# Attention plus quantised feed-forward on one core: another place for the streamed tiles, an earlier end of the search for the largest product, and another order of roundings

## Chip, core and metric

One core of a Trainium2 chip runs the whole kernel in one launch. The metric is the device time of a run in microseconds; each kernel is timed by the median of its runs.

## The reference

x is (2, 2048, 512), that is 4096 rows of 512. A cross-attention with 128 context rows per batch is added to it, then a feed-forward block whose activations and weights are rounded to integers and scaled back:

```python
x = x + xattn(layernorm(x), ctx_1024, Wq, Wkv)
x = x + ffn(layernorm(x), w_gate, w_up, w_down)

def ffn(x, w_gate, w_up, w_down):
    x = act_qdq(x)                            # 16 bit, one scale over the whole tensor
    up = act_qdq(x @ lpbq_dequant(w_up).T)    # weights: 4 bit, a scale per block of 32
    gate = act_qdq(x @ lpbq_dequant(w_gate).T)
    sig = fixed_qdq_u16(sigmoid(gate))
    gate = act_qdq(gate * sig)
    o = act_qdq(gate * up)
    return o @ lpbq_dequant(w_down).T
```

`act_qdq` takes the largest magnitude of its whole operand, divides by 32767 and rounds. The hidden width is 1536. Each of these scales has to be known before the rounding that uses it, and that cuts the work into stages.

## The kernel before

**Stages.** (1) Norm and attention, in 8 groups of 512 rows (`NG = 8`, `TG = 512`); it leaves the normalised rows, transposed, in `hT`. (2) Gate: per group, 12 chunks of 128 hidden columns. (3) Up: the groups in reverse order, again 12 chunks each; a tile j (0 to 23) is a third of a group, 4 chunks, and has two half tiles c = 2j and 2j+1. (4) Down: 32 units m of 128 rows, two to a tile t of 256 rows.

**Numbers in parts.** TensorE works on exact integers: an activation integer is split into a high and a low part and a third combination (`split_integers`), and so is a weight. A chunk in gate or up is `project`: 8 matmuls of 128x512 into q and 4 into e, with the weights stationary and the activation parts (`parts_g`, `parts_u`) streamed. In down the roles change: the product's parts (`o_parts`) are stationary and the down weights `wd[f]`, f = 0 to 11, are streamed, 24 matmuls into q (L865) and 12 into e (L873).

**Homes.** Group t has its parts in `homes[t % 2]`: `homes[0]` is a pool `parts0` on the left side of SBUF, `homes[1]` is `parts1`, 24 KB per partition and the outermost pool on the right side. In down `homes[1]` holds the weights 0 to 3 (`first_wd`). Ahead of `parts1`, `hT` (64 KB) has stood at that place, and ahead of it `prep0`. The x tiles (`xp`, 4 of 8 KB), the integers `hi` (32 KB) and up's tiles (`keep`: three u of 8 KB and three p of 4 KB) are on the left.

**Up.** Per tile j ACT makes the sigmoid of a later gate tile in three passes (L609 to L611), DVE makes the integers p (L647). Per half tile ACT takes q out of PSUM (L715), DVE subtracts e (L716), the half is stored to `up_d`, and `bound` (ACT L655, DVE L656) takes the largest magnitude of u times p into a column of `pumax`. Only the tile holding the largest of these can hold the largest rounded product. So `fetch_best` finds, per partition, the row of the best half tile, and fetches u and p of it from DRAM with two indirect DMAs (L673). This covers half tiles 0 to 46; half tile 47 is rounded itself. When the scale of u is known (`r_u`, L762), both are rounded (L772), multiplied and reduced (L774), an all-reduce over the partitions follows (L779), and then the scale of the product is known. A flag (L915) says whether the bound was sure; otherwise a general path (not entered here) follows.

**Down.** ACT rounds u to integers (`round_up`, L828); DVE makes the product's integer and its parts (`round_o`, L850, L851, L853, and ACT's cast L854, then `third_part`, L857); TensorE multiplies; `finish_first` (L878, L880) and `finish` (L884) scale, add x and store. The first group's u and p are still on the chip. Later groups load p (L812) and u (`load_up`, L801) from DRAM; u goes into the same three tiles, so a load waits for the last `round_up` that reads them.

**Order.** Each engine runs its queue in order, as laid down by the program's planner at build time. `in_order` adds pairs of instructions of one engine that keep their order without a semaphore; `high_priority` puts a piece ahead in the plan. SP issues nearly all DMAs, in order; POOL issues the two indirect ones. In the first group of down each unit's rounding is made one unit ahead:

```python
if m + 1 < NS * NU:
    ...
    in_order(casts[-1], *round_up(uis[t], tiles_u, t, j * P, P))
    if m + 2 == NS * NU:
        tiles_u = load_up(groups[1])
```

Of the kernel before, what the change touches and what calls it, by code (L numbers as in the profile page):

```python
# [76 lines left out]
def tile_xattn_ffn(  # L77
# [56 lines left out]
    pumax = const.tile([P, NH - 1], F32, name="pumax")  # L134
# [109 lines left out]

    with ExitStack() as c0:

        with ExitStack() as c1:
            prep = c1.enter_context(tc.tile_pool(name="prep", bufs=1))
            xp = c1.enter_context(tc.tile_pool(name="xp", bufs=4))
# [251 lines left out]
        hi_pool = c0.enter_context(tc.tile_pool(name="hi", bufs=1))  # L501
        hi = hi_pool.tile([P, ND, NT], I16, name="hi")
# [20 lines left out]
        with ExitStack() as c2:  # L523
            wg = [load_parts(wg_d, f, "wg") for f in range(NF)]
            s_h, r_h = act_scale(*over_partitions(hmax, name="h"), "h")

            unit = const.tile([P, 1], F32, name="unit")
            nc.vector.tensor_scalar(unit, s_h, BASE, None, ALU.mult)
            wk1 = c2.enter_context(tc.tile_pool(name="wkb1", bufs=1))
            for c in range(ND):  # L530
                nc.vector.tensor_scalar(hi[:, c, :TG], hT[:, c, :TG], r_h, QMAX, ALU.mult, ALU.min)
            first = split_integers(wk1, homes[0], hi[:, :, :TG], [ND, TG], "g0", ND)

            table = const.tile([P, 1], F32, name="table")
            nc.scalar.activation(table, unit, AF.Sigmoid)
            for t in range(1, NG):
                if t % 2:
                    nc.vector.tensor_scalar(hi[:, :, ts(t, TG)], hT[:, :, ts(t, TG)], r_h, QMAX, ALU.mult, ALU.min)
                else:
                    nc.scalar.activation(hi[:, :, ts(t, TG)], hT[:, :, ts(t, TG)], AF.Copy, scale=r_h)  # L540
            hpool.__exit__(None, None, None)
            home1 = tc.tile_pool(name="parts1", bufs=1, side="right")
            homes.append(ctx.enter_context(home1))
            wk2 = c2.enter_context(tc.tile_pool(name="wkb2", bufs=2))
            wpp = c2.enter_context(tc.tile_pool(name="wprep", bufs=1))
            ps_m = c2.enter_context(tc.tile_pool(name="ps_m", bufs=3, space=PSUM))
            ps_t = c2.enter_context(tc.tile_pool(name="ps_t2", bufs=2, space=PSUM))

            steps = chain(split_rows(wpp, ps_t, w_up, wu_d, "u"), split_down(wpp, ps_t))
            groups, wu = {}, []  # L550
            for t in range(NG):
                if t == 0:
                    parts = first
                else:
                    parts = split_integers(wk1, homes[t % 2], hi[:, :, ts(t, TG)], [ND, TG], f"g{t}")
# [24 lines left out]
    keep = ctx.enter_context(tc.tile_pool(name="keep", bufs=NK))  # L580

    with ExitStack() as c3:
# [70 lines left out]
        def bound(c, u, pi):  # L653
            ua = wk2.tile([P, 2, TG], F32, tag="ua", name=f"ua_{c}")
            magnitudes = nc.scalar.activation(ua, u, AF.Abs)  # L655
            nc.vector.tensor_tensor_reduce(ua, ua, pi, 1.0, 0.0, ALU.mult, ALU.max, pumax[:, c : c + 1])  # L656
            return magnitudes

        kept_u, kept_p = [], []
        best = const.tile([P, 8], F32, name="best")  # L660

        def fetch_best():
# [5 lines left out]
            to_row = nc.vector.scalar_tensor_tensor(row, where[:, 0:1], float(P), lane, ALU.mult, ALU.add)  # L668
            fetched = []
            for src, dt in ((up_d, F32), (p_d, I16)):  # L670
# [5 lines left out]
                    in_=src[: NH - 1].rearrange("n p i t -> (n p) (i t)"),  # L676
# [3 lines left out]
            return to_row, *fetched  # L680
# [10 lines left out]
        for j, (t, k) in enumerate(order):  # L691
# [13 lines left out]
            kept_u.append(u4)  # L705
            for h in range(2):
# [3 lines left out]
                if c + 1 < NH:  # L710
# [5 lines left out]
                    nc.vector.tensor_tensor(u4[:, both, :], u4[:, both, :], e, ALU.subtract)  # L716
                else:
                    for i in range(2):
# [4 lines left out]
                        in_order(magnitudes, nc.scalar.activation(v, q, AF.Copy, scale=1.0 + 1.0 / BASE))  # L723
                        in_order(to_row, nc.vector.tensor_tensor(v, v, e, ALU.subtract))
# [42 lines left out]
        two = const.tile([P, 3], F32, name="two")  # L767
        last = [v[:, 2:, :].rearrange("p i t -> p (i t)") for v in (u4, pi)]
        rounded = []
        for i, (uv, pv) in enumerate([last, (ub, pb)]):  # L770
# [3 lines left out]
            nc.vector.tensor_tensor_reduce(product, ui, pv, 1.0, 0.0, ALU.mult, ALU.max, two[:, i : i + 1])  # L774
            if i == 0:
                nc.vector.tensor_scalar(two[:, 2:3], best[:, 1:2], r_u, 1.0 + 2.0**-18, ALU.mult, ALU.mult)
                nc.vector.tensor_scalar(two[:, 2:3], two[:, 2:3], 0.5 * (QMAX + 2.0), None, ALU.add)
        top = const.tile([P, 3], F32, name="top")
        nc.gpsimd.partition_all_reduce(top, two, P, bass_isa.ReduceOp.max)  # L779


    with ExitStack() as c5:
# [14 lines left out]
        def load_up(g):  # L797
            tiles = []
            for k in range(NK):
                u4 = keep.tile([P, NQ, TG], F32, tag="u4", name=f"u5_{g}_{k}")  # L800
                nc.sync.dma_start(  # L801
                    out=u4.rearrange("p (h c) t -> p h c t", h=2), in_=up_d[rows_of(g, k)].rearrange("h p c t -> p h c t")
                )
                tiles.append(u4)
            return tiles
# [19 lines left out]
        def round_up(ui, tiles, t, at=0, width=TD):  # L825
# [4 lines left out]
                    tiles[k][:, :, ds(t % NS * TD + at, width)],  # L830
# [76 lines left out]
        tiles_u, kept_p = kept_u[-NK:], kept_p[-NK:]  # L907
        uis = {0: up_integers(0)}
        in_order(rounded[0], *round_up(uis[0], tiles_u, 0, 0, P))
        scale_of_pu()  # L910
        a_o = const.tile([P, 1], F32, name="a_o")
        nc.vector.tensor_tensor(a_o, top[:, 0:1], top[:, 1:2], ALU.max)
        flag = const.tile([P, 1], I32, name="flag")
        with tc.high_priority():
            nc.vector.scalar_tensor_tensor(flag, top[:, 2:3], floor, a_o, ALU.max, ALU.is_le)  # L915
# [57 lines left out]
        for m in range((last + 1) * NU + 2):  # L973
# [4 lines left out]
            if m <= last * NU + NU - 1:  # L978
# [66 lines left out]
```

## Time and profile before

| what | value |
|---|---|
| median of 3 runs | 1023.36 us (1021.37 to 1025.08) |
| profiled execution | 1021.18 us, its span 1019.4 us |
| PE busy | 953.6 us (94%) |
| DVE, ACT, POOL busy | 806.2, 549.4, 90.4 us |
| granted TensorE clock, mean | 0.975 |
| DMA, mean | 259 GB/s |

Norm and attention take up to about 177 us, gate to about 457, up to 726, down from 743 to the end. In a line of the timeline the columns are the start and the length in us, the engine, the line of the kernel, the operation, the tile written and the tiles read, shapes, a count of merged instructions, and in square brackets the idle time of the engine just before and what ended it. In a line of the waits they are the waiting engine and line, what it waited for, the total in us, how often, and the longest.

### The profile page before, as it was taken

The numbers are of one execution on the slowest core, as the hardware profiler recorded it, in microseconds if no ns is written. First come the engines' busy times: TensorE is split into PE (matmuls) and PEld (weight loads), VectorE is DVE, ScalarE is ACT, GpSimd is POOL, SyncE is SP. The second block draws the span as 40 slices with busy tenths as digits, with TensorE's granted clock in tenths as the row PEclk, the third lists the DMA queues.
The fourth block names the chain that finished last, engine by engine and source line by source line (L and its number), as shares of the span: only waits on it lengthen the run. The fifth ranks groups of instructions, "written<-read, shape, count | busy, mean of one in ns | idle before, by whom it ended". The sixth has DMA issues, their size and how long they took to land. (4 is left out here: it accounts for less than half of the span.)

```text
span 1019.4 us, 11685 instructions
## 1 busy us (share of the span) xinstructions
PE 953.6 (94%) x4321; PEld 764.6 (75%) x4321; DVE 806.2 (79%) x1000; ACT 549.4 (54%) x655; POOL 90.4 (9%) x67
## 2 busy tenths in 40 slices
PE   6998874999999999999999999999488999999998
PEld 5765642888888888878888888888367888888886
DVE  4589865999997989546996997987688997777772
ACT  2268786432333323218997998887255444444331
POOL 0101111000000000000000000000011322222221
PEclk9999997999999999999999999999789999999999
DMA  9187644886895775797997997897946576654711
GB/s 340 32 313 270 253 176 173 332 336 271 311 383 186 300 226 195 254 387 274 352 348 292 344 370 293 334 378 249 393 145 253 185 244 227 237 189 154 243 66 42
DMA packets 103596, 263.72 MB, mean 259 GB/s; under 512 B 6064, under 2 KB 46000, under 8 KB 94832
## 3 DMA queue, kind: packets, MB, share of 16 engines
q1 hardware_dynamic: 102496, 259.02, 68.8%
q0 software_dynamic: 512, 2.88, 0.7%
q10 hardware_dynamic: 528, 1.05, 0.3%
q8 instruction: 34, 0.56, 0.2%
q14 instruction: 26, 0.21, 0.1%
HBM read 136.05 MB, written 126.88 MB: 258 GB/s over the span
## 5 line engine op out<-in xcount | busy, mean ns | idle before, releaser
L517 PE MATMUL q_g<-parts_g,wg 128*128 128x512 f32 x768 | 196.4, 396 | 5.1 <-ACT parts_g L236 5.1
L517 PEld LDWEIGHTS q_g<-parts_g,wg 128*128 128x128 f32 x768 | 144.5, 189 | 38.0 <-ACT parts_g L236 5.5
L568 ACT ACTIVATE g<-q_g 128x512 f32<-128x512 f32 x96 | 57.2, 598 | 182.0 <-PE q_g L517 179.2
L517 PE MATMUL q_u<-parts_u,wu 128*128 128x512 f32 x576 | 144.6, 393 | 0.3 <-ACT u L715 0.3
L517 PEld LDWEIGHTS q_u<-parts_u,wu 128*128 128x128 f32 x576 | 108.2, 188 | 25.2 <-ACT u L715 0.7
L865 PE MATMUL yq<-wd,o_parts 128*128 128x512 f32 x512 | 122.1, 391 | 0.0
L865 PEld LDWEIGHTS yq<-wd,o_parts 128*128 128x128 f32 x512 | 96.6, 189 | 21.1
L521 PE MATMUL e_g<-parts_g,wg 128*128 128x512 f32 x384 | 106.8, 396 | 0.0
L569 DVE CUSTOM_DVE_ANT_0 g<-g,e_g 128x512 f32<-128x512 f32 x96 | 64.8, 681 | 39.2 <-PE e_g L521 38.7
L865 PE MATMUL yq<-first_wd,o_parts 128*128 128x512 f32 x256 | 68.3, 411 | 20.4 <-ACT o_parts L854 20.4
L878 ACT ACTIVATE yqs<-yq,q_o 128x512 f32<-128x512 f32 x32 | 22.0, 687 | 119.1 <-PE yq L865 119.1
L521 PEld LDWEIGHTS e_g<-parts_g,wg 128*128 128x128 f32 x384 | 72.2, 189 | 16.3 <-DVE parts_g L238 0.4
L880 POOL TENSOR_TENSOR qx<-yqs,x 128x512 f32<-128x512 f32 x32 | 64.5, 2016 | 210.6 <-ACT yqs L878 152.0
L521 PE MATMUL e_u<-parts_u,wu 128*128 128x512 f32 x288 | 78.2, 393 | 0.0
L865 PEld LDWEIGHTS yq<-first_wd,o_parts 128*128 128x128 f32 x256 | 50.1, 196 | 32.7 <-ACT o_parts L854 21.0
L857 DVE SCALAR_TENSOR_TENSOR o_parts<-sa,oi 128x1536 fp32r<-128x1536 int16 (+2 forms) x41 | 58.2, 1438 | 19.9 <-PE ye L873 19.9
L656 DVE CUSTOM_DVE_ANT_0 ua<-ua,pi 128x1024 f32<-128x1024 f32 x47 | 57.1, 1220 | 18.8 <-ACT ua L655 18.6
L853 DVE SCALAR_TENSOR_TENSOR o_parts<-sa,oi 128x1536 fp32r<-128x1536 int16 (+2 forms) x41 | 58.6, 1430 | 14.9 <-PE yq L865 13.0
L854 ACT CAST o_parts<-sa 128x1536 fp32r<-128x1536 int16 (+2 forms) x41 | 48.8, 1190 | 34.4 <-DVE sa L851 34.4
L716 DVE TENSOR_TENSOR u<-u,e_u 128x1024 f32<-128x1024 f32 x47 | 57.0, 1217 | 12.4 <-ACT u L715 12.3
L873 PE MATMUL ye<-wd,o_parts 128*128 128x512 f32 x256 | 64.0, 392 | 0.0
L647 DVE SCALAR_TENSOR_TENSOR pi<-gi,k_p,sq 128x2048 int16<-128x2048 int16 x24 | 56.4, 2349 | 9.6 <-ACT sq L611 9.6
(185 smaller groups left out, 1554.5 us busy)
## 6 DMA issues: line engine op xcount, KB each, us to landing
gate_d<-g SPq DMA_DIRECT2D x24, 1024.0 KB, 6.5
up_d<-u SPq DMA_DIRECT2D x48, 512.0 KB, 7.3
gt<-gate_d SPq DMA_DIRECT2D x22, 1024.0 KB, 8.3
u<-up_d SPq DMA_DIRECT2D x21, 1024.0 KB, 6.5
parts_d<-parts_g SPq DMA_DIRECT2D x6, 3072.0 KB, 11.1
parts_u<-parts_d SPq DMA_DIRECT2D x6, 3072.0 KB, 13.4
p_d<-pi SPq DMA_DIRECT2D x24, 512.0 KB, 9.7
p<-p_d SPq DMA_DIRECT2D x84, 128.0 KB, 3.1
```

What stands on the lines that cost most here:

```text
L517: nc.tensor.matmul(q, lhsT=w[:, s, c, :], rhs=parts[:, s, c, :], start=(c + s == 0), stop=(c + s == ND))
L521: nc.tensor.matmul(e, lhsT=w[:, 2, c, :], rhs=parts[:, 2, c, :], start=(c == 0), stop=(c == ND - 1))
L568: nc.scalar.activation(g4[:, i, :], q, AF.Copy, scale=1.0 + 1.0 / BASE)
L569: nc.vector.tensor_tensor_reduce(g4[:, i, :], g4[:, i, :], e, 1.0, LOWEST, ALU.subtract, ALU.max, gtop[:, m : m + 1])
L647: nc.vector.scalar_tensor_tensor(pi, gi, k_p, sq, ALU.mult, ALU.mult)
L656: nc.vector.tensor_tensor_reduce(ua, ua, pi, 1.0, 0.0, ALU.mult, ALU.max, pumax[:, c : c + 1])
L716: nc.vector.tensor_tensor(u4[:, both, :], u4[:, both, :], e, ALU.subtract)
L853: made.append(nc.vector.scalar_tensor_tensor(parts[1][:, c], sa[:, c], -BASE, oi[:, c], ALU.mult, ALU.add))
L857: return nc.vector.scalar_tensor_tensor(parts[2][:, c], sa[:, c], BASE + 1.0, oi[:, c], ALU.mult, ALU.subtract)
L865: nc.tensor.matmul(q, lhsT=parts[s][:, f, :], rhs=wd[f][:, s, :], start=(f + s == 0), stop=(f + s == NF))
L873: nc.tensor.matmul(e, lhsT=parts[2][:, f, :], rhs=wd[f][:, 2, :], start=(f == 0), stop=(f == NF - 1))
L880: nc.gpsimd.tensor_tensor(qx, qs, x1[:, m % NU, :], ALU.add)
```

## The change

x, the integers `hi` and up's tiles get a common pool `far` of four tiles of 8 KB on the right side, opened ahead of all others there, so it is the outermost. `prep0`, `hT` and `parts1` now lie inside it, 32 KB further from the end. Two p tiles share the fourth `far` tile; the third stays in `keep`. The tiles of u are three fixed ones that are written again and again, in up and by `load_up`.

The search for the best product now covers half tiles 0 to 45; the last tile's two halves, 46 and 47, are both rounded from the chip. The search and fetch follow half tile 45, and the subtraction (L716) of half tile 46 comes behind the row on DVE. The older order of half tile 47's instructions behind them goes. The loads of the third parts of the weights 0 to 3 move to the end of up, behind the last store.

In down, unit 0 rounds the second half of tile 0 and then the whole of tile 1, and after that each tile's first unit rounds the next tile. `load_up` of the second group is issued in unit 0 instead of unit 2.

```diff
-    pumax = const.tile([P, NH - 1], F32, name="pumax")
+    pumax = const.tile([P, NH - 2], F32, name="pumax")
...
+    far = ctx.enter_context(tc.tile_pool(name="far", bufs=4, side="right"))
+
+    def far_tile(name):
+        return far.tile([P, NJ * D], F32, tag="far", name=name)
...
-            xp = c1.enter_context(tc.tile_pool(name="xp", bufs=4))
...
-                xt = xp.tile([P, NJ, D], F32, tag="xt", name=f"xt_{g}")
+                xt = far_tile(f"xt_{g}").rearrange("p (j d) -> p j d", j=NJ)
...
-        hi_pool = c0.enter_context(tc.tile_pool(name="hi", bufs=1))
-        hi = hi_pool.tile([P, ND, NT], I16, name="hi")
+        his = [far_tile(f"hi_{i}").bitcast(I16).rearrange("p (t c k) -> p t c k", t=2, c=ND) for i in range(NG // 2)]
+        hi = [his[t // 2][:, t % 2] for t in range(NG)]
...
-    keep = ctx.enter_context(tc.tile_pool(name="keep", bufs=NK))
+    keep = ctx.enter_context(tc.tile_pool(name="keep", bufs=1))
+    tiles_u = [far_tile(f"u4_{i}").rearrange("p (i t) -> p i t", i=NQ) for i in range(NK)]
+    two_p = far_tile("pi_01").bitcast(I16).rearrange("p (n i t) -> p n i t", n=2, i=NQ)
+    kept_p = [two_p[:, 0], two_p[:, 1], keep.tile([P, NQ, TG], I16, name="pi_2")]
...
-            pi = keep.tile([P, NQ, TG], I16, tag="pi", name=f"pi_{j}")
-            kept_p.append(pi)
+            pi = kept_p[j % NK]
...
-                    in_=src[: NH - 1].rearrange("n p i t -> (n p) (i t)"),
+                    in_=src[: NH - 2].rearrange("n p i t -> (n p) (i t)"),
...
-            u4 = keep.tile([P, NQ, TG], F32, tag="u4", name=f"u4_{j}")
+            u4 = tiles_u[j % NK]
...
-                    nc.vector.tensor_tensor(u4[:, both, :], u4[:, both, :], e, ALU.subtract)
+                    less = nc.vector.tensor_tensor(u4[:, both, :], u4[:, both, :], e, ALU.subtract)
+                    if c + 2 == NH:
+                        in_order(row_known, less)
...
-                        in_order(magnitudes, nc.scalar.activation(v, q, AF.Copy, scale=1.0 + 1.0 / BASE))
-                        in_order(to_row, nc.vector.tensor_tensor(v, v, e, ALU.subtract))
+                        nc.scalar.activation(v, q, AF.Copy, scale=1.0 + 1.0 / BASE)
+                        nc.vector.tensor_tensor(v, v, e, ALU.subtract)
...
-                if c + 2 < NH:
+                if c + 3 < NH:
                     bound(c, u4[:, both, :], pi[:, both, :])
-                elif c + 2 == NH:
+                elif c + 3 == NH:
                     with tc.high_priority():
-                        magnitudes = bound(c, u4[:, both, :], pi[:, both, :])
-                        to_row, ub, pb = fetch_best()
+                        bound(c, u4[:, both, :], pi[:, both, :])
+                        row_known, (ub, pb) = fetch_best()
...
-            if t == 0 and k == 1:
-                load_down(range(NE), slice(2, 3))
-
-        rest = load_down(range(NE + NQ, NF), slice(0, 2)) + load_down(range(NE, NF), slice(2, 3))
+
+        rest = load_down(range(NE + NQ, NF), slice(0, 2)) + load_down(range(NF), slice(2, 3))
         in_order(stored, *rest)
...
-        last = [v[:, 2:, :].rearrange("p i t -> p (i t)") for v in (u4, pi)]
+        there = [(u4[:, ts(h, 2), :].rearrange(flat), pi[:, ts(h, 2), :].rearrange(flat)) for h in range(2)]
         rounded = []
-        for i, (uv, pv) in enumerate([last, (ub, pb)]):
+        for i, (uv, pv) in enumerate([*there, (ub, pb)]):
...
-        nc.vector.tensor_tensor(a_o, top[:, 0:1], top[:, 1:2], ALU.max)
+        nc.vector.tensor_reduce(a_o, top[:, 0:3], AX.X, ALU.max)
...
-                if m + 1 < NS * NU:
-                    t, j = divmod(m + 1, NU)
-                    if j == 0:
-                        uis[t] = up_integers(t)
-                    in_order(casts[-1], *round_up(uis[t], tiles_u, t, j * P, P))
-                    if m + 2 == NS * NU:
-                        tiles_u = load_up(groups[1])
-                elif t < last and j == (NU - 1 if t + 1 == NS else 0):
+                if m == 0:
+                    in_order(casts[-1], *round_up(ui, 0, P, P))
+                if j == 0 and t < last:
                     uis[t + 1] = up_integers(t + 1)
-                    in_order(casts[-1], *round_up(uis[t + 1], tiles_u, t + 1))
+                    in_order(casts[-1], *round_up(uis[t + 1], t + 1))
                     if t % NS == NS - 2 and t + NS <= last:
-                        tiles_u = load_up(groups[t // NS + 1])
+                        load_up(groups[t // NS + 1])
```

More of the change, by code (lines that the diff above doesn't have):

```diff
@@ L530, in tile_xattn_ffn @@
             for c in range(ND):
-                nc.vector.tensor_scalar(hi[:, c, :TG], hT[:, c, :TG], r_h, QMAX, ALU.mult, ALU.min)
-            first = split_integers(wk1, homes[0], hi[:, :, :TG], [ND, TG], "g0", ND)
+                nc.vector.tensor_scalar(hi[0][:, c], hT[:, c, :TG], r_h, QMAX, ALU.mult, ALU.min)
+            first = split_integers(wk1, homes[0], hi[0], [ND, TG], "g0", ND)
             table = const.tile([P, 1], F32, name="table")
@@ L537, in tile_xattn_ffn @@
                 if t % 2:
-                    nc.vector.tensor_scalar(hi[:, :, ts(t, TG)], hT[:, :, ts(t, TG)], r_h, QMAX, ALU.mult, ALU.min)
+                    nc.vector.tensor_scalar(hi[t], hT[:, :, ts(t, TG)], r_h, QMAX, ALU.mult, ALU.min)
                 else:
-                    nc.scalar.activation(hi[:, :, ts(t, TG)], hT[:, :, ts(t, TG)], AF.Copy, scale=r_h)
+                    nc.scalar.activation(hi[t], hT[:, :, ts(t, TG)], AF.Copy, scale=r_h)
             hpool.__exit__(None, None, None)
@@ L554, in tile_xattn_ffn @@
                 else:
-                    parts = split_integers(wk1, homes[t % 2], hi[:, :, ts(t, TG)], [ND, TG], f"g{t}")
+                    parts = split_integers(wk1, homes[t % 2], hi[t], [ND, TG], f"g{t}")
                 if t < NG - 2:
@@ L654, in bound @@
             ua = wk2.tile([P, 2, TG], F32, tag="ua", name=f"ua_{c}")
-            magnitudes = nc.scalar.activation(ua, u, AF.Abs)
+            nc.scalar.activation(ua, u, AF.Abs)
             nc.vector.tensor_tensor_reduce(ua, ua, pi, 1.0, 0.0, ALU.mult, ALU.max, pumax[:, c : c + 1])
-            return magnitudes
-        kept_u, kept_p = [], []
         best = const.tile([P, 8], F32, name="best")
@@ L667, in fetch_best @@
             row = const.tile([P, 1], U32, name="row")
-            to_row = nc.vector.scalar_tensor_tensor(row, where[:, 0:1], float(P), lane, ALU.mult, ALU.add)
+            known = nc.vector.scalar_tensor_tensor(row, where[:, 0:1], float(P), lane, ALU.mult, ALU.add)
             fetched = []
@@ L679, in fetch_best @@
                 fetched.append(v)
-            return to_row, *fetched
+            return known, fetched
         def load_down(fs, part=slice(None)):
@@ L701, in tile_xattn_ffn @@
                     load_down(range(NE), slice(0, 2))
-            u4 = keep.tile([P, NQ, TG], F32, tag="u4", name=f"u4_{j}")
+            u4 = tiles_u[j % NK]
             if j:
                 pi = integers_of_p(j)
-            kept_u.append(u4)
             for h in range(2):
@@ L765, in tile_xattn_ffn @@
         nc.vector.tensor_scalar(s_u, s_u, 1.0 / QMAX, TINY, ALU.mult, ALU.max)
-        two = const.tile([P, 3], F32, name="two")
-        last = [v[:, 2:, :].rearrange("p i t -> p (i t)") for v in (u4, pi)]
+        most = const.tile([P, 4], F32, name="most")
+        flat = "p i t -> p (i t)"
+        there = [(u4[:, ts(h, 2), :].rearrange(flat), pi[:, ts(h, 2), :].rearrange(flat)) for h in range(2)]
         rounded = []
-        for i, (uv, pv) in enumerate([last, (ub, pb)]):
+        for i, (uv, pv) in enumerate([*there, (ub, pb)]):
             ui = wk3.tile([P, NQ, TG], I16, tag="gi", name=f"ui_b{i}").rearrange("p i t -> p (i t)")[:, : 2 * TG]
@@ L773, in tile_xattn_ffn @@
             product = wk2.tile([P, 2 * TG], F32, tag="ua", name=f"product_b{i}")
-            nc.vector.tensor_tensor_reduce(product, ui, pv, 1.0, 0.0, ALU.mult, ALU.max, two[:, i : i + 1])
+            nc.vector.tensor_tensor_reduce(product, ui, pv, 1.0, 0.0, ALU.mult, ALU.max, most[:, i : i + 1])
             if i == 0:
[L776 to L779, printed above, removed]
+                nc.vector.tensor_scalar(most[:, 3:4], best[:, 1:2], r_u, 1.0 + 2.0**-18, ALU.mult, ALU.mult)
+                nc.vector.tensor_scalar(most[:, 3:4], most[:, 3:4], 0.5 * (QMAX + 2.0), None, ALU.add)
+        top = const.tile([P, 4], F32, name="top")
+        nc.gpsimd.partition_all_reduce(top, most, P, bass_isa.ReduceOp.max)
     with ExitStack() as c5:
@@ L797, in load_up @@
         def load_up(g):
-            tiles = []
             for k in range(NK):
-                u4 = keep.tile([P, NQ, TG], F32, tag="u4", name=f"u5_{g}_{k}")
                 nc.sync.dma_start(
-                    out=u4.rearrange("p (h c) t -> p h c t", h=2), in_=up_d[rows_of(g, k)].rearrange("h p c t -> p h c t")
-                )
-                tiles.append(u4)
-            return tiles
+                    out=tiles_u[k].rearrange("p (h c) t -> p h c t", h=2),
+                    in_=up_d[rows_of(g, k)].rearrange("h p c t -> p h c t"),
+                )
         def load_p(t):
@@ L823, in up_integers, with round_up @@
             return wki.tile([P, NF, TD], I16, tag="ui5", name=f"ui5_{t}")
-        def round_up(ui, tiles, t, at=0, width=TD):
+        def round_up(ui, t, at=0, width=TD):
             return [
@@ L829, in round_up @@
                     ui[:, ts(k, NQ), ds(at, width)],
-                    tiles[k][:, :, ds(t % NS * TD + at, width)],
+                    tiles_u[k][:, :, ds(t % NS * TD + at, width)],
                     AF.Copy,
@@ L905, in scale_of_o @@
             nc.vector.tensor_scalar(e_o, s_o, -BASE, None, ALU.mult)
-        tiles_u, kept_p = kept_u[-NK:], kept_p[-NK:]
         uis = {0: up_integers(0)}
-        in_order(rounded[0], *round_up(uis[0], tiles_u, 0, 0, P))
+        in_order(rounded[0], *round_up(uis[0], 0, 0, P))
         scale_of_pu()
         a_o = const.tile([P, 1], F32, name="a_o")
-        nc.vector.tensor_tensor(a_o, top[:, 0:1], top[:, 1:2], ALU.max)
+        nc.vector.tensor_reduce(a_o, top[:, 0:3], AX.X, ALU.max)
         flag = const.tile([P, 1], I32, name="flag")
         with tc.high_priority():
-            nc.vector.scalar_tensor_tensor(flag, top[:, 2:3], floor, a_o, ALU.max, ALU.is_le)
+            nc.vector.scalar_tensor_tensor(flag, top[:, 3:4], floor, a_o, ALU.max, ALU.is_le)
         scale_of_o(a_o)
```

## Prediction

> **What bounds the kernel now.** I read the page first, then the PE waits, then PE's timeline group by group, then the timeline of the two places where PE stands still. The page:
>
> ```profile
> span 1019.4 us, 11685 instructions
> PE 953.6 (94%) x4321; PEld 764.6 (75%) x4321; DVE 806.2 (79%) x1000; ACT 549.4 (54%) x655; POOL 90.4 (9%) x67
> PEclk9999997999999999999999999999789999999999
> ```
>
> From 180 us on PE is busy in nearly every slice and its granted clock is full; the exception is near slices 29 to 31 (720 to 785 us). So two things count: the time of one matmul, and what stops PE there. The PE waits name the second; the two stops are 17.1 and 3.2 us:
>
> ```profile
> PE yq L865 <- ACT o_parts L854: 20.4, 2, 17.1
> ```
>
> The first is in PE's timeline. Here is a group whose streamed operand `parts_u` lies in `homes[1]` (t = 1), then one where it lies in `homes[0]` (t = 0). Columns: start us, us.
>
> ```profile
> 665.30 2.04 PE L517 MATMUL q_u<-parts_u,wu 128*128 128x512 f32 x8
> ...
> 668.11 2.03 PE L517 MATMUL q_u<-parts_u,wu 128*128 128x512 f32 x8
> ```
>
> ```profile
> 696.06 1.98 PE L517 MATMUL q_u<-parts_u,wu 128*128 128x512 f32 x8
> ...
> 698.78 1.98 PE L517 MATMUL q_u<-parts_u,wu 128*128 128x512 f32 x8
> ```
>
> The step from one chunk of 12 matmuls to the next (8 of q, 4 of e) is 2.81 us in the odd group and 2.72 us in the even one: 234 against 227 ns a matmul, with the same shapes, full clock and no wait. The weights are the same `wu`; only the home differs. The gate pass shows it too: t = 1 steps from 216.12 to 218.92 (2.80), t = 0 from 192.62 to 195.34 (2.72). In down, where `first_wd` (weights 0 to 3) lies in `homes[1]`:
>
> ```profile
> 808.38 2.03 PE L865 MATMUL yq<-first_wd,o_parts 128*128 128x512 f32 x8
> 810.25 3.81 PE L865 MATMUL yq<-wd,o_parts 128*128 128x512 f32 x16
> ...
> 816.66 2.03 PE L865 MATMUL yq<-first_wd,o_parts 128*128 128x512 f32 x8
> ```
>
> The eight on `first_wd` take 1.87 us (234 ns each), the next 16 take 3.64 (227); a unit of 36 takes 8.28 us, where 36 at 226.7 would take 8.16. So every matmul that streams from `homes[1]` costs some 7 ns (in down, 10 per such matmul) more.
>
> **The change part by part.**
>
> (a) The move. `parts1` (24 KB) is the outermost tile on the right side now; afterwards the four `far` tiles (32 KB) lie outside it, so it ends 32 KB further in. If the slow zone ends there, odd groups run like even ones: gate 4 groups x 12 chunks x 0.08 = 3.8 us; up 48 x 0.09 = 4.3; down 32 units x 0.12 = 3.8. Together 11.9 us, all on the path since PE has no wait in these stages. No row shows f32r data streamed from between the even home and the odd one, so the bounds are 11.9 and 0 (the zone reaches further in). [...] The rows say 234 against 227, so the address or something tied to it matters[...]. [...] I take 11.9.
>
> What replaces it at the end is x, `hi`, u and two tiles of p, which DVE, ACT and DMA touch; PE reads only x there, as the stationary operand of 128 transposes in the first 160 us, where PE waits for others anyway (0). ACT already writes to the right side without loss: L461 into `hT` (64 KB there) takes 991 to 1038 ns for 128x1024, L715 into u on the left 999 to 1029. So 0 for them. The two p tiles in one buffer, u without new tiles and x, `hi`, u sharing buffers all wait for readers one stage or three tiles back: 0, covered by 10.9 us of PE per tile.
>
> The loads of `wg` no longer lie on x's place; they start at 168.78 because the last x was still in use, and can now start some 6 us earlier. PE starts at 176.76 on the chain of maxima and finds its weights: 0.
>
> (b) The end of up. Between the last matmul (723.5) and the first of down:
>
> ```profile
> 729.99 1.07 POOL L673 DMA_INDIRECT best<-up_d,row  x1 [270.09 <-DMA wd<-wd_d]
> 731.37 0.97 POOL L673 DMA_INDIRECT best<-p_d,row  x1 [0.30 <-issue]
> 737.00 1.15 ACT L772 ACTIVATE ui_b<-best,r_u 128x1024 int16<-128x1024 f32 x1 [8.75 <-DMA best<-up_d,row]
> 738.18 1.22 DVE L774 CUSTOM_DVE_ANT_0 product_b<-ui_b,best 128x1024 f32<-128x1024 int16 x1 [8.67 <-ACT ui_b L772]
> ...
> 739.51 0.38 POOL L779 PARTITION_ALL_REDUCE top<-two  x1 [7.17 <-DVE two L774]
> ...
> 742.14 0.48 DVE L850 SCALAR_TENSOR_TENSOR oi<-pi,k_o,ui 128x256 int16<-128x256 int16 x1 [1.17 <-DVEq L918]
> ...
> 743.43 3.78 PE L865 MATMUL yq<-first_wd,o_parts 128*128 128x512 f32 x8 [17.14 <-ACT o_parts L854]
> ```
>
> The gather needs half tile 46 in `up_d`; that store was issued at 720.6 and landed at 729.1, and the gather went out 0.9 later. Now the search stops at half tile 45 (store issued 715.5, landed 723.0) and p of tile 22 (landed 720.6); its row is known by 719, where L656 for 45 ended at 718.9. So the gather goes out at 723.9, 6.1 us earlier. With the same 7.0 us to land it is there at 730.9. Meanwhile r_u is ready at 727.1 and ACT rounds the two halves on the chip: 2 x 1.15, to 729.4. The added half costs 1.15 on ACT and 1.22 on DVE, both under that landing; without that cover, 1.2. Then 1.15 + 1.22 for the fetched one, ending 6.1 us before 739.4. What follows (4.0 us to PE) is unchanged. If the gather lands sooner, ACT's own three roundings end at 730.55 and the gain stops at 7.6; if it meets the `wd` loads as hard as before and loses 2 more, 4. I take 6.1. The bound on 46 that goes (1.05 ACT, 1.22 DVE) lay ahead of the last maxima; L724's order behind the search is gone as well, but the 2.28 us maximum of tile 22 then falls later: 0, at best 0.7. On SP four loads (the third parts of weights 0 to 3, 1 MB) move from 715.9 behind the last store; the queue carries the same bytes, the last load ended at 742.1, and PE needs third parts only 7.5 us after its start (about 744.8): 0, and 1 to 2 if they come last.
>
> (c) Order of roundings in down. The second stop:
>
> ```profile
> 775.12 1.15 ACT L828 ACTIVATE ui<-u,r_u 128x1024 int16<-128x1024 f32 x1 [1.04 <-DMA u<-up_d]
> ...
> 776.31 2.51 DVE L850 SCALAR_TENSOR_TENSOR oi<-p,k_o,ui 128x1536 int16<-128x1536 int16 x1 [1.76 <-ACT ui L828]
> ...
> 780.44 1.47 ACT L854 CAST o_parts<-sa 128x1536 fp32r<-128x1536 int16 x1 [3.59 <-DVE sa L851]
> ...
> 781.96 3.60 PE L865 MATMUL yq<-first_wd,o_parts 128*128 128x512 f32 x8 [3.23 <-ACT o_parts L854]
> ```
>
> u of the second group was loaded from 764.8 and landed at 775.1, because its tiles were free only after unit 2 rounded. Now tile 1 is rounded whole in unit 0, so the loads go out at about 753 and land by 763; tile 2 is rounded in unit 2. Then L850 starts at 774.5, when L884 ends, not at 776.3, and later units show 1.81, 0.56 and 1.48 for L850, L851, L854: cast done by 778.4, PE free at 778.7. The 3.2 us go. The half clock behind it goes too: eight matmuls took 3.60 us against 2.03. [...] the row shows the loss, so the row counts: 1.6. Together 4.8. The price: in unit 0 ACT rounds 3 x 1.13 more ahead of unit 1's casts, first cast then at 753.1 + 0.6 = 753.7, where PE starts unit 1 at 753.73: 0, up to 1. What is late next is that cast. SP's other loads (p, x1, `out`) queue behind u loads that wait until 753; p is needed at 774: 0.
>
> **Sum.** 11.9 + 6.1 + 4.8 = 22.8. The profiled execution took 1021.2 us (span 1019.4 and 1.8 around it), 2.2 below the median 1023.4. So 998.4 by its time, 1000.6 by the median; I say 1000.
>
> **The rivals.**
> 1. The slow zone reaches further in than 32 KB, or goes with something else than the end: (a) is 0, and 1023.4 - 10.9 = 1012.5. For it: nothing shows its edge. Against: only the outermost tile is slow, everything else PE streams runs at 227.
> 2. The gather or the first casts of down eat most of (b) and (c): the gather lands with the `wd` loads at 735, or unit 1 waits 3 us for ACT. (a) and some 5 remain: 1006.
> 3. Slower: ACT becomes the bound of up, since its accesses to u at the end are slow as PE's are. Per tile ACT has 1.99 + 2.00 + 1.90 + 2 x 1.01 + 2 x 1.05 = 10.0 us, PE will have 4 x 2.72 = 10.9. The 4.1 us on u would have to grow by a fifth to bind, and by 45% (1.8 us a tile, over 24 tiles) to cost more than the 22.8 won; at 60% it is about 1032. Against: L461 above.
> 4. It doesn't do what it says: DVE, busy for 49.3 of the 50 us from 250 to 300, holds the odd gate groups, so (a) loses 1 to 2: 1002, within the first forecast.
>
> **How the numbers follow.** All three gains: 0.68, 995 to 1006. Rival 1: 0.17, 1009 to 1015. Rival 2: 0.10, 1004 to 1009. Rival 3: 0.03. No gain at all, for reasons unseen: 0.02. To leave out no more than 2 in 10 the range takes in rival 2 and most of rival 1: 994 to 1013. About 0.3% (3 us) is what a measurement can tell; faster 0.95, within 0.02, slower 0.03.
>
> **What would show it.** (a): odd groups step 2.72 per chunk, units of down 8.16; steps of 2.81 mean rival 1. (b): the gather goes out within a microsecond of the last up matmul (now 6.5 us behind it), and PE's wait at L865 is near 11 us, not 17. (c): no second wait at L865, eight matmuls of unit 4 in 2.0 us. L715 and L655 above 1.1 us would mean rival 3. A new PE wait in unit 1 for L854, or for a `wd` load, would make (b) or (c) wrong.

## The result, and the profile after

The changed kernel takes 1015.56 us (median of 4 runs, 1014.48 to 1017.45), the one before 1023.68 in the same comparison: ratio 0.9925, 95% interval 0.9899 to 0.9951. That is 8.1 us less, where 23 were forecast, and above the stated range of 994 to 1013. The profiled execution took 1017.45 us with a span of 1015.7; it is the longest of the four.

The page after the change:

```profile
span 1015.7 us, 11683 instructions
PE 954.7 (94%) x4321; PEld 764.9 (75%) x4321; DVE 808.0 (80%) x1000; ACT 548.5 (54%) x652; POOL 88.3 (9%) x67
PEclk9999896899999999999999999999979999999999
```

PE is as busy as before, although it had been expected to need 12 us less for the same matmuls. PE's timeline of an odd group (t = 1, `homes[1]` now 32 KB inside the end) says why:

```profile
670.60 2.04 PE L522 MATMUL q_u<-parts_u,wu 128*128 128x512 f32 x8
...
673.41 2.03 PE L522 MATMUL q_u<-parts_u,wu 128*128 128x512 f32 x8
```

The step is 2.81 us as before, and the units of down still take 8.28. Part (a) brought nothing.

The gains lie in the two stops. The two PE waits at L868 (before, one line with 20.4 us):

```profile
PE yq L868 <- DMA first_wd<-wd_d: 11.9, 1, 11.9
...
PE yq L868 <- ACT o_parts L857: 1.6, 1, 1.6
```

From up to down, on the timeline:

```profile
728.98 1.07 POOL L679 DMA_INDIRECT best<-up_d,row  x1 [265.33 <-DMA p_d<-pi]
730.36 0.97 POOL L679 DMA_INDIRECT best<-p_d,row  x1 [0.30 <-issue]
...
734.85 1.15 ACT L778 ACTIVATE ui_b<-best,r_u 128x1024 int16<-128x1024 f32 x1 [0.87 <-DMA best<-up_d,row]
...
737.97 1.23 DVE L780 CUSTOM_DVE_ANT_0 product_b<-ui_b,best 128x1024 f32<-128x1024 int16 x1 [2.62 <-DMA best<-p_d,row]
...
742.88 3.78 PE L868 MATMUL yq<-first_wd,o_parts 128*128 128x512 f32 x8 [11.89 <-DMA first_wd<-wd_d]
```

The last up matmul starts at 728.4; the gather goes out 0.6 us behind it, where it was 6.9 before. PE resumes at 742.9: the start-to-start stop is 14.45 us, before it was 20.30. PE's bracket names a load of `first_wd`, but those were the third parts, which PE needs only at 750. What PE waited for is ACT's cast into `o_parts`, ready at 742.82, 0.06 us before PE went on, as PE's weight load has it (`LDWEIGHTS`, idle 12.08 until ACT L857).

The second stop, at unit 4, is gone, and a smaller one has come at unit 3:

```profile
764.65 1.15 ACT L831 ACTIVATE ui<-u,r_u 128x1024 int16<-128x1024 f32 x1 [1.05 <-DMA u<-up_d]
...
767.16 1.15 ACT L831 ACTIVATE ui<-u,r_u 128x1024 int16<-128x1024 f32 x1 [1.36 <-DMA u<-up_d]
...
769.74 1.15 ACT L831 ACTIVATE ui<-u,r_u 128x1024 int16<-128x1024 f32 x1 [1.43 <-DMA u<-up_d]
...
771.45 2.14 PE L868 MATMUL yq<-first_wd,o_parts 128*128 128x512 f32 x8 [1.58 <-ACT o_parts L857]
```

Three times ACT stands in its queue for a part of u, and unit 3's casts stand behind it.

### The profile page after: what moved, and what is told of

It reads as the page before. It is cut to its first block, busy times and chain, and to the rows that moved or that the text cites. A ratio compares the mean times of both kernels' runs of the same rounds, so it can differ in the third digit from the quotient of the medians.

```text
span 1015.7 us, 11683 instructions
## 1 busy us (share of the span) xinstructions
PE 954.7 (94%) x4321; PEld 764.9 (75%) x4321; DVE 808.0 (80%) x1000; ACT 548.5 (54%) x652; POOL 88.3 (9%) x67
## 3 DMA queue, kind: packets, MB, share of 16 engines
q10 hardware_dynamic: 528, 1.05, 0.3%
## 5 line engine op out<-in xcount | busy, mean ns | idle before, releaser
L522 PE MATMUL q_g<-parts_g,wg 128*128 128x512 f32 x768 | 198.5, 398 | 5.1 <-ACT parts_g L236 5.1
L868 PE MATMUL yq<-wd,o_parts 128*128 128x512 f32 x512 | 122.1, 391 | 0.0
L868 PEld LDWEIGHTS yq<-wd,o_parts 128*128 128x128 f32 x512 | 96.5, 188 | 21.1
L883 POOL TENSOR_TENSOR qx<-yqs,x 128x512 f32<-128x512 f32 x32 | 62.4, 1950 | 209.1 <-ACT yqs L881 182.7
L868 PE MATMUL yq<-first_wd,o_parts 128*128 128x512 f32 x256 | 66.9, 404 | 13.5 <-DMA first_wd<-wd_d 11.9
L860 DVE SCALAR_TENSOR_TENSOR o_parts<-sa,oi 128x1536 fp32r<-128x1536 int16 (+2 forms) x41 | 60.7, 1499 | 18.5 <-PE ye L876 18.5
L856 DVE SCALAR_TENSOR_TENSOR o_parts<-sa,oi 128x1536 fp32r<-128x1536 int16 (+2 forms) x41 | 59.5, 1451 | 14.0 <-PE yq L868 11.8
L857 ACT CAST o_parts<-sa 128x1536 fp32r<-128x1536 int16 (+2 forms) x41 | 48.6, 1189 | 37.1 <-DVE sa L854 37.1
L868 PEld LDWEIGHTS yq<-first_wd,o_parts 128*128 128x128 f32 x256 | 49.0, 192 | 25.5 <-ACT o_parts L857 14.1
```

Of the source, the lines that this page charges most:

```text
L522: nc.tensor.matmul(q, lhsT=w[:, s, c, :], rhs=parts[:, s, c, :], start=(c + s == 0), stop=(c + s == ND))
L856: made.append(nc.vector.scalar_tensor_tensor(parts[1][:, c], sa[:, c], -BASE, oi[:, c], ALU.mult, ALU.add))
L860: return nc.vector.scalar_tensor_tensor(parts[2][:, c], sa[:, c], BASE + 1.0, oi[:, c], ALU.mult, ALU.subtract)
L868: nc.tensor.matmul(q, lhsT=parts[s][:, f, :], rhs=wd[f][:, s, :], start=(f + s == 0), stop=(f + s == NF))
L883: nc.gpsimd.tensor_tensor(qx, qs, x1[:, m % NU, :], ALU.add)
```

## The experiments

### Why the odd groups are slow: three theories, four pads

Theory 1: the start address of the streamed tile decides, in steps of some bytes. Theory 2: there is a slow zone with its edge further in. Theory 3: operands that lie far apart are slow. An unused tile (a pad) on the right side moves all the tiles there by a few bytes:

```diff
+    edge = ctx.enter_context(tc.tile_pool(name="edge", bufs=1, side="right")).tile([P, 32], mybir.dt.uint8, name="edge")
+    nc.gpsimd.memset(edge, 0)
     far = ctx.enter_context(tc.tile_pool(name="far", bufs=4, side="right"))
```

**right32**, as above. 

> The changed kernel with an unused tile of 32 bytes per partition outermost on the right side, so that everything on the right side starts 32 bytes earlier (homes[1] then starts on a multiple of 64 bytes, as homes[0] does; now it starts 32 bytes off one). Theory 1 (the start address decides[...]): odd groups step 2.72 us per chunk of 12 matmuls, a unit of down takes 8.16 us, and the run is about 11 to 12 us faster than the changed kernel, near 1004. Theory 2 (a slow zone that reaches further in than 32 KB): 32 bytes change nothing, odd groups stay at 2.80, 1015 to 1016. Theory 3 (operands far apart in SBUF are slow): as theory 2.

**right96**, 96 bytes. 

> The same with 96 bytes, so that homes[1] starts on a multiple of 128 bytes, while homes[0] stays 64 bytes off one. If lines of 64 bytes are all there is, odd groups step 2.72 us as with 32 bytes, and the run is near 1004. If lines of 128 bytes count too[...], odd groups become faster than even ones[...]. A slow zone: no change, 1015.

**right64**, 64 bytes. 

> The control: 64 bytes, so that homes[1] is moved inward but is again 32 bytes off a multiple of 64. Theory 1: odd groups stay at 2.80 us per chunk, 1015. If any small move helps, they fall to 2.72. Theories 2 and 3: 2.80.

**left32**, a tile of 32 bytes on the left side ahead of `parts0` instead. 

> The changed kernel with an unused tile of 32 bytes just ahead of homes[0] on the left side, so that homes[0] is 32 bytes off a multiple of 64 as homes[1] is. Theory 1: even groups rise from 2.72 to 2.80 us per chunk, in all 8 groups about 8 us slower, near 1023; down's units do not change, since what they stream lies ahead of the pad. Theories 2 and 3: even groups stay at 2.72, 1015.

Measured: right32 1015.39 us (median of 5; ratio to before 0.9918, 0.9902 to 0.9935), right96 1010.34, right64 1016.89, left32 1022.81 (one run each). PE's timeline of the same odd group (t = 1) in right96, then of an even one (t = 2) in left32:

```profile
664.94 1.99 PE L524 MATMUL q_u<-parts_u,wu 128*128 128x512 f32 x8
...
667.68 1.99 PE L524 MATMUL q_u<-parts_u,wu 128*128 128x512 f32 x8
```

```profile
637.68 2.03 PE L524 MATMUL q_u<-parts_u,wu 128*128 128x512 f32 x8
...
640.48 2.03 PE L524 MATMUL q_u<-parts_u,wu 128*128 128x512 f32 x8
```

In right96 odd groups step 2.74 to 2.75, in left32 even groups step 2.80 instead of 2.72; in right32 and right64 odd groups stay at 2.80. So a few bytes decide, and not the zone or the distance: theories 2 and 3 are out. But theory 1 missed right32, where 2.72 was expected. Lines of 64 bytes, a guess of the author's, are not the rule either, since by them right96 too was to step 2.72; nor are lines of 128, by which its odd groups were to be faster than even ones. left32 missed in one more place: down's units were to stay at 8.28, but every second one takes 8.38, the one whose stationary `o_parts` lies in `homes[0]`, though what it streams did not move. That was a first sign that the stationary tile counts as well.

### The cost by itself

**sweep** issues only such chunks, with chosen start addresses, three chunks for each pair:

```python
    CONFIGS.append((100 * KB + m, 8 * KB))       # the streamed tile moves
...
    CONFIGS.append((100 * KB + m, 8 * KB + m))   # both by the same
...
    CONFIGS.append((100 * KB, 8 * KB + w))       # the weights alone
...
    CONFIGS.append((a * KB, 8 * KB))             # far apart
...
```

> None of the reference's work is done here: only the chunk of 12 matmuls (8 into q, 4 into e, f32r, weights 128x128, 512 columns streamed), three chunks for each of 49 pairs of start addresses of the streamed and the stationary tile. First the streamed tile is moved by 0 to 1536 bytes, then both tiles by the same, then the weights alone, then the streamed tile to places from 16 to 175 KB beyond the first byte, then both far apart. What is measured is the mean step from matmul to matmul. Theory 1 (the streamed tile's start address): the step depends on the streamed tile's offset alone, not on the weights', and not on the place. Theory 1b[...]: the step depends on the difference of the two offsets, and moving both by the same changes nothing. Theory 2 (a slow zone): offsets of some bytes do nothing, places beyond some edge between 100 and 175 KB cost 7 ns. Theory 3 (distance): 7 ns from some distance on, in both directions.

PE's timeline, in this order: equal starts; the streamed tile 32 bytes on; both 64 bytes on; the weights alone 32 bytes on; the streamed tile 175 KB into the room (the one tile that holds all operands) instead of 100. The step to the next row of x8 is what counts.

```profile
48.42 1.98 PE L98 MATMUL q<-room 128*128 128x512 f32 x8
...
51.14 1.98 PE L98 MATMUL q<-room 128*128 128x512 f32 x8
...
56.58 2.03 PE L98 MATMUL q<-room 128*128 128x512 f32 x8
```

```profile
183.99 1.98 PE L98 MATMUL q<-room 128*128 128x512 f32 x8
...
186.71 1.98 PE L98 MATMUL q<-room 128*128 128x512 f32 x8
```

```profile
225.02 2.03 PE L98 MATMUL q<-room 128*128 128x512 f32 x8
...
227.82 2.03 PE L98 MATMUL q<-room 128*128 128x512 f32 x8
```

```profile
364.69 1.98 PE L98 MATMUL q<-room 128*128 128x512 f32 x8
...
367.41 1.98 PE L98 MATMUL q<-room 128*128 128x512 f32 x8
```

The steps are 2.72, 2.72, 2.80 and 2.72; from 56.58 the trace goes on with 59.39 and 62.19, 2.80. Over all 49 pairs the step follows, to within about 1 ns a matmul, from the streamed start less the stationary one, modulo 256 bytes. The table has the ns per matmul in the sweep (the second and third chunk of a pair with the streamed tile moved; the first, behind the change of pair, differs by up to 3 ns), and what the kernels show in the groups that have that difference. The traces hold no addresses. As the program is built, the weights start at 64 modulo 256 in all these kernels, `homes[0]` too (96 in left32), and `homes[1]` at 224 before and after the change; a pad on the right side takes its bytes off the 224.

| difference | sweep | kernel |
|---|---|---|
| 0 | 226.7 | even groups, 226.7 |
| 32 | 233.3 | left32, even groups, 233.3 |
| 64 | 228.9 | right96, odd groups, 228.9 |
| 96 | 233.3 | right64, odd groups, 233.3 |
| 128 | 233.3 | right32, odd groups, 233.3 |
| 160 | 234.4 | before and after, odd groups, 234.3 |
| 192, 224 | 233.3, 233.3 | |
| 256, 512, 1024 | 226.7, 226.7, 226.7 | |

At difference 0 every place from 16 to 175 KB gives 226.7. Theory 1b of the expectation, called theory 4 from here on, has it right that the difference counts: 2.80 with either tile alone 32 bytes on, 2.72 with both 64 on. And 32 KB, by which the change moves `homes[1]`, is a multiple of 256.

**sweep_fine** takes smaller steps. 

> As the first sweep, without the reference's work: the streamed tile in steps of 4 to 16 bytes against fixed weights, then both by the same, then pairs with equal differences. Theory 4 with a granule of 64 bytes: differences of 4 to 24 bytes cost as much as 32 (233 ns), whatever their size; with a granule of 16 bytes: differences of 4 to 12 cost something, 16, 32 and 48 are alike. Equal differences give equal steps: (64, 128) as (0, 64), 233 ns, (128, 64) as (64, 0), 229 ns. At 0 and 256 it is 226.7; whether any difference is below that is open.

Equal differences of 32-byte multiples agree again: (64, 128) gives 233.3, (128, 64) 228.9. Below that grain neither expectation held: 4 bytes give 237.7, 12 bytes 229.2, 16 bytes 231.7, and both tiles 4 or 48 bytes on, which leaves the difference at 0, gives 237.6 and 233.4. So the rule of the difference is shown for starts at multiples of 32 bytes, as these kernels' tiles have. No difference was faster than 0.

### The pad that the rule asks for

**right160** is the changed kernel with a pad of 160 bytes, **before160** the kernel before with the same pad and nothing else.

> The changed kernel with an unused tile of 160 bytes per partition outermost on the right side. homes[1] then starts at the same remainder of 256 bytes (64) as homes[0] and all weights and stationary parts; as the changed kernel stands the streamed tile is at 224 and the weights at 64. Theory 4, from the sweep (the step depends on the difference of the streamed and the stationary start, modulo 256 bytes, and is least at 0): all groups step 2.72 us per chunk, a unit of down takes 8.16, and 11 to 12 us go against the changed kernel: 1003 to 1005. Theory 1 (the streamed start alone) is out by the sweep; by it 32 bytes would have been enough, and 160 would give the same 1015.

> The kernel before with the same unused tile of 160 bytes outermost on the right side and nothing else: homes[1] stays at the very end of SBUF. Theory 4: odd groups 2.72, units of down 8.16, 11 to 12 us less than before: 1011 to 1012. Theory 2 (a slow zone at the end): nothing changes, 1023.

right160: 1006.8 us (1006.15 to 1009.28), ratio to before 0.9833 (0.9819 to 0.9847). before160: 1012.02 us against 1024.21, ratio 0.988 (0.9863 to 0.9897). An odd group (t = 1) of right160, then of before160:

```profile
663.99 1.98 PE L524 MATMUL q_u<-parts_u,wu 128*128 128x512 f32 x8
...
666.71 1.98 PE L524 MATMUL q_u<-parts_u,wu 128*128 128x512 f32 x8
```

```profile
664.93 1.98 PE L519 MATMUL q_u<-parts_u,wu 128*128 128x512 f32 x8
...
667.65 1.98 PE L519 MATMUL q_u<-parts_u,wu 128*128 128x512 f32 x8
```

All groups step 2.72 and units of down take 8.16 in both. before160 keeps `homes[1]` at the end of SBUF, but for the 160 bytes, and gains 12.2 us by the medians, what part (a) was said to be worth; the place does not matter. (The two profiled executions differ by 5.4 only: that of before160 is its slowest of four, that of before is among its fastest.) right160 gains 8.8 on the changed kernel, less than the 11 to 12 expected, and its profile shows where some of it went again: group 5 of gate takes 37.8 us against 36.9, and the first group of up 35.7 against 34.9. PE waits 1.9 us in the first, where it waited 1.4, and behind that wait its granted clock is 0.50 from 378 to 380 us (1.00 behind the one of 1.4). In the second it waits 3.4 where it waited 1.9.

### One part of the change undone at a time

**no_move**: the pool on the left.

```diff
-    far = ctx.enter_context(tc.tile_pool(name="far", bufs=4, side="right"))
+    far = ctx.enter_context(tc.tile_pool(name="far", bufs=4))
```

> The changed kernel with the pool far on the left side, at the place where it is opened: x, integers and u lie on the left, and parts1 is at the very end of SBUF as before. The two other parts of the change stay. If the move brings nothing (odd groups step 2.80 us in both places): 1015 to 1016, as the changed kernel. If the move costs something in gate and up, where the first profile of the changed kernel is 5.3 us longer than the one of before up to the last matmul of up: 1010 to 1012. If it gained what was forecast: 1027.

**no_order**: the roundings of down as before.

```diff
-                if m == 0:
-                    in_order(casts[-1], *round_up(ui, 0, P, P))
-                if j == 0 and t < last:
+                if m + 1 < NS * NU:
+                    t, j = divmod(m + 1, NU)
...
+                    in_order(casts[-1], *round_up(uis[t], t, j * P, P))
+                    if m + 2 == NS * NU:
+                        load_up(groups[1])
+                elif t < last and j == (NU - 1 if t + 1 == NS else 0):
```

> The changed kernel with the order of roundings in down as before (each unit's rounding one unit ahead in the first group, u of the second group loaded in unit 2). Units 2 to 4 took 8.28 + 11.67 + 9.86 us before and 10.03 + 8.37 + 8.28 after, so 3.1 us are expected to come back: 1018 to 1019. If the order was worth the forecast 4.8: 1020.4.

**no_search**: the search to half tile 46, the third parts loaded where they were.

```diff
-                    in_=src[: NH - 2].rearrange("n p i t -> (n p) (i t)"),
+                    in_=src[: NH - 1].rearrange("n p i t -> (n p) (i t)"),
...
-                elif c + 3 == NH:
+                elif c + 2 == NH:
...
-        rest = load_down(range(NE + NQ, NF), slice(0, 2)) + load_down(range(NF), slice(2, 3))
+        rest = load_down(range(NE + NQ, NF), slice(0, 2)) + load_down(range(NE, NF), slice(2, 3))
...
```

> The changed kernel with the search over half tiles 0 to 46 as before, the third parts of weights 0 to 3 loaded where they were, and one half tile rounded from the chip. The stop between up and down should be 20.3 us as before instead of 14.5: 1021 to 1022. If the earlier search is hidden by the loads of the down weights, 1016.

| kernel | median us | ratio to before | interval |
|---|---|---|---|
| changed | 1015.56 | 0.9925 | 0.9899 to 0.9951 |
| no_move | 1015.80 | 0.9930 | 0.9903 to 0.9958 |
| no_order | 1020.06 | 0.9960 | 0.9945 to 0.9974 |
| no_search | 1020.33 | 0.9971 | 0.9960 to 0.9983 |

By the ratios the move is worth 0.5 us, within the intervals nothing; the order of roundings 3.6; the earlier search 4.7; each of these differences is uncertain by some 3 us. The traces are sharper. In no_order units 2 to 4 of down take 32.2 us, where they take 26.7 in the changed kernel and 29.8 before. The PE waits of no_search have the old stop back; its stop start to start is 20.2 us:

```profile
PE yq L869 <- ACT o_parts L858: 17.2, 2, 17.0
```

### A version that beats both

**best** is right160 with two more edits:

```diff
-                if j == 0 and t < last:
+                if t < last and j == (NU - 1 if t + 1 == NS else 0):
...
-            if t == 0 and k == 0:
+            if t == 0 and k == 1:
                 load_down(range(NE, NE + NQ), slice(0, 2))
```

> As right160, and two more edits: tile 2 is rounded in unit 3 instead of unit 2 (behind the landing of u, so that unit 3's casts don't wait for it: 1.6 us of PE's wait and the slow matmuls behind it go), and the four loads of the down weights 4 to 7 come one tile of up later, behind the store of half tile 45, which then lands some 5 us earlier, so that the gather can start when its row is known and the stop between up and down falls from 14.5 to about 12 us. Expected: 1.7 and 2.5 us below right160, about 1000. If the later loads of the weights end too late, PE waits for them in the first unit of down and the second gain is lost.

1003.15 us (1002.79 to 1004.31), ratio to before 0.9796 (0.9783 to 0.9809), 3.7 us below right160 where 4.2 were expected. The gather now goes out before the end of up, and both stops of PE stand in one line of the waits:

```profile
PE yq L870 <- ACT o_parts L859: 10.4, 2, 9.6
```

The stop start to start is 12.2 us. The small stop was moved rather than taken away: units 3 and 4 take 9.15 and 9.27 us instead of 8.16, because tile 2, rounded after u has landed at 763.7, is now late for unit 4.

## Why the prediction was wrong, point by point

**(a), 11.9 us: the size of what could be had was right, the cause wrong.** The step that failed is "If the slow zone ends there, odd groups run like even ones". There is no slow zone: before160 steps 2.72 us with `homes[1]` at the end but for 160 bytes. The rows (2.81 against 2.72) differed in two things, the place and the start address, and "only the home differs" took them for one. `homes[1]` starts at 224 modulo 256 bytes and the weights at 64, and moving by 32 KB left that as it was. That removing the excess is worth some 12 us, before160 shows with 12.2. That a zone would end where the move puts `homes[1]` was the author's estimate, which no row showed, and the chance of 0.68 that rested on it was too high. With 512 columns every time, the step is 226.7 to 234.4 ns (sweep, starts at multiples of 32 bytes), not by where the rows lie, but by how their start lies to that of the weights. That is shown for matmuls each with its own weights; why the two starts matter to each other stays open.

**(b), 6.1 us: right.** The stop shrank by 5.85. The gather went out 0.6 us behind the start of the last matmul, forecast within one. Its u landed in 5.8 us, but its p, which the forecast had left out, in 7.5, and p ended the wait (DVE at 737.97, not ACT). That the sum came out so close is in part luck: the fetched product began 9.5 us behind the last matmul's start, where the forecast has 8.9, and what follows it to PE took 4.9 where it had taken 5.3. By the medians the search is worth 4.7; the next paragraph has the rest.

**(c), 4.8 us: mechanism right, 3.1 came.** Units 2 to 4 took 29.81 us before and 26.67 after. The term that failed is "the loads go out at about 753 and land by 763", which is 9.6 and 19.6 us behind PE's first matmul of down (743.43). In the changed kernel u went out 14.5 us behind it, the last of it landed at 769.7, 26.8 behind it, and ACT's rounding of tile 2 held up unit 3's casts:

```profile
757.34 2.61 SPq L805 DMA_DIRECT2D u<-up_d  x3
```

The reason is that (b) and (c) were summed as if they did not touch. SP issues the loads of the down weights, waits at a branch (L920) until they have landed, 4.7 us in the changed kernel (its last semaphore there at 749.1 us, the last load issued at 743.3 and a median of 5.7 us from issue to landing) and 1.5 in no_search, and only then issues ten loads of p and those of u. (b) lets PE begin down nearly 6 us earlier, but the weights come no earlier: SP issued their last load at 743.3, behind PE's start at 742.88. no_search has the new order of roundings without (b), the moved loads of third parts included. There SP issued the last weight load at 739.2, PE began at 746.07, and u went out 8.0 us behind that, with the same ten loads of p ahead of it, which the forecast had behind it:

```profile
754.11 1.72 SPq L806 DMA_DIRECT2D u<-up_d  x3
...
766.83 3.23 ACT L832 ACTIVATE ui<-u,r_u 128x1024 int16<-128x1024 f32 x3
```

ACT rounds tile 2 there without a wait, and units 2 to 4 take 25.5 us, 4.3 less than before, near the forecast. So (b) took some 1.2 us from (c), and 5.8 less 1.2 is about what the medians give for the search. The half clock did go: the new 1.6 us stop is followed by eight matmuls in 2.14 us at a granted clock of 1.00 (771 to 773 us), while the 3.2 us stop before was followed by 3.60 us, the clock at 0.50 from 782 to 784. (A short stop is not always spared: right160 has 0.50 behind 1.9 us.) The forecast named a late cast as the next thing, but in unit 1, where there was no wait.

**What was not in the sum.** In the two profiled executions the stretch up to the last matmul of up is 5.3 us longer after the change, which is why the spans differ by only 3.7 while (b) and (c) give 9.0. Of the 5.3, 0.9 lie ahead of gate, 2.9 in gate and 1.5 in up. Group 5 of gate takes 36.9 us against 35.3; PE waits 1.4 us there for transposes of the down weights, and goes on when DVE has written their input. no_move shows the same (36.6), no_order and no_search too, before160 does not (35.2). So it comes with the changed program and not with the place of the tiles; which edit makes the planner order gate so was not tried. Part of the 5.3 can be the spread between executions: the changed kernel's runs lie 3 us apart, and by the medians 8.1 of the 9.0 remain.

**The rivals.** Rival 1, with (a) at 0, came nearest, and by its second reading, that the cost "goes with something else than the end"; its first, a zone that reaches further in, is out. The 3 us above its 1012.5 are the 1.7 missing in (c) and the longer gate and up. Rival 2 did not come: the gather's u landed in 5.8 us, and unit 1 took 8.28. Rival 3 is out: ACT's instructions on u kept their lengths, with medians of 1.01 us (L720) and 1.05 (L663). (Its time for 60% comes to about 1039 by its own numbers, not 1032.) Rival 4 could not show while (a) brought nothing; in right160, where (a) is to be had, PE's longest stop within gate is in an odd group, for what DVE makes.

## What to carry to other kernels

When the same matmul takes longer in one group than in another, list everything in which the operands differ, the start address modulo small powers of two included, before naming a zone; a sweep of start addresses in a kernel of its own settled it here in one run. In these kernels tiles that are streamed and tiles that are loaded as weights should start at the same remainder of 256 bytes (sweep: 226.7 ns at difference 0, 228.9 to 234.4 at 32 to 224); 160 unused bytes, added to the kernel before, brought 12.2 us, where the whole change brought 8.1. Two gains on one path need not add up (here (b) took some 1.2 us from (c)): who shortens a stop should look at which transfers have so far ended inside it, and what waits in the same queue behind them.

## What the runs showed of the hardware

For f32r matmuls of 128x512, each with its own 128x128 weights, the step from one to the next was 226.7 ns when streamed and stationary tile start at the same remainder of 256 bytes, 228.9 when the streamed one starts 64 further on, and 233.3 to 234.4 at differences of 32, 96, 128, 160, 192 and 224 (sweep). The kernel before, at a granted clock of 1.00 from 655 to 687 and from 688 to 719 us, had 234.3 in the odd group there and 226.7 in the even one. No place tried changed it: at difference 0 the streamed tile had 226.7 from 16 to 175 KB into the room (sweep), and before160 streams from the last 25 KB at 226.7. At starts that are not multiples of 32 bytes the step was up to 237.7, even at difference 0 (sweep_fine). PE's clock was granted at half behind stops of 3.2 us (before, 0.50 from 782 to 784 us) and 1.9 us (right160, 0.50 from 378 to 380), and stayed full behind stops of 1.6 and 1.4 us in the changed kernel (1.00 from 771 to 775 and from 380 to 382).
